# Graph attention block: bulk loading of the first chunks, query projections as jobs, and another place for the exponential

## Chip, core and metric

The kernel runs on one core of one Trainium2 chip. The metric is the device time of one execution in microseconds (us), the median over several runs. Each engine (PE for matrix products, DVE, ScalarE = ACT, GpSimd = POOL, and SP, which here only issues transfers) has a queue of its own and takes its instructions strictly in the order in which the program wrote them; semaphores hold an instruction until what it needs is there.

## What is computed

Eight frames of 2048 nodes with 256 channels go through one attention block in which a node sees only its neighbours, all in float32:

```python
qkv = einsum('fnc,ck->fnk', x, w_qkv); q, k, v = split(qkv, 3)     # 8 heads of 32 channels
scores = einsum('fnhd,fmhd->fhnm', q, k) / sqrt(32)
scores = where(adj > 0, scores, -1e9)                              # adj: 2048 x 2048, the same for all frames and heads
t = einsum('fhnm,fmhd->fnhd', softmax(scores), v)
y = layernorm(x + t);  z = relu(y @ w1 + b1) @ w2 + b2
out = layernorm(x + layernorm(y + z))
```

## The kernel before

**Tiles and items.** A frame is cut in 4 chunks of 512 queries (`qc`), the heads in 2 groups of 4 (`g`), the keys in 16 blocks of 128 (`mb`). The main loop (L418) runs over the 8 x 4 x 2 x 16 = 1024 items (f, qc, g, mb), one step for each. The 16 steps of one (f, qc, g) are here called a group; there are 64.

**One item.** `scores` (L202) takes a buffer `pt` of 128 x 4 x 512 from the pool `pp` (10 buffers) and two of three pairs of PSUM banks, issues the score products of four heads (L210, PE), adds the mask (L213, DVE, two instructions of 128 x 1024) and takes the exponential in place (L215, ACT, one instruction of 128 x 2048). `values` (L219) multiplies with V (L227, PE) into a bank `O` that collects a whole group; at the last item of a group it copies that bank to SBUF (L231, ACT). `add_up` (L240) sums the exponentials for the softmax denominators, six items of a group on POOL (L247) and six by accumulating transfers that POOL issues (L244). Scores run two items ahead: step t issues `scores(items[t + 2])`, then `values(items[t])`, then `add_up(items[t])` (L431 to L439).

**Jobs.** All other work of the loop comes as generators in the list `fill`, ordered by a due step (`start`, L368). At every step but the first of a group, `advance` (L373) lets them go on before the scores are issued, in order of their due steps; in a step only one piece of work that needs a PSUM bank is allowed (`yield BANK`), `yield n` puts a job off by n steps, and a job that loads waits until so many of the three input buffers (`live`, L96) are free; where one waits for them, no job behind it may load. The bank that a job gets (`bank`, L85) is, in the main loop, the one of two that the running group does not use as `O`: after a group's end that is the bank that L231 empties. The jobs are: the mask of the next query chunk (`mask_ahead`, L394, built of `turn_mask`, L113, in the first frame only; later frames reload masks), the turn of x for the next frame (`turn`, L148: load, transpose, store the turned chunk `xT` to DRAM as `XD`, project the queries), K and V (`project`, L176, which reloads `XD`), denominators (L271), outcome (L300) and tail (L319: layer norms and the two dense layers, with L328, L339, L349, L351).

**The start.** Before the loop, for each chunk c of frame 0 (L405): `turn` (with its queries), `project` for heads 0 to 3, `turn_mask`, which loads the adjacency block in two halves, converts each on DVE (L122), transposes (L132) and evicts with a minimum (L133). These take their buffers from the three input buffers. Then `project` for heads 4 to 7 for all chunks, from `xT` reloaded from `XD` (L182), and the scores of the first two items.

**Constants.** Weights, bias columns and rows are loaded from ACT's queue (L597 to L605) ahead of everything else on it. The identity matrix for the transposes is made on POOL (L619), which also adds two rows (L617). In this part, outside of `fast_path`, the framework may order instructions of an engine by when their operands are there; in `fast_path` the program's order stands.

Of the kernel before, what the change touches and what calls it, by code (L numbers as in the profile page):

```python
# [10 lines left out]
F32 = mybir.dt.float32  # L11
BF16 = mybir.dt.bfloat16
I32 = mybir.dt.int32
F8 = mybir.dt.float8e5
AF = mybir.ActivationFunctionType
ALU = mybir.AluOpType
AX = mybir.AxisListType

P = 128
H = 8  # L20
D = 32
CH = 512
# [6 lines left out]
BANK, TURNED, ROOM, INPUTS = -1, -2, -3, -10  # L29
# [24 lines left out]
def fast_path(ctx, tc, cst, x, adj, out, RS):  # L54
# [30 lines left out]
    def bank(dt=F32):  # L85
        shape = [P, CH] if dt == F32 else [P, 2, CH]
        if state["side"] is not None:
            i = 1 - state["side"]
            return ps_x[i].tile(shape, dt, name=f"x{i}")
        i = state["turn"]  # L90
        state["turn"] = (i + 1) % 5
        pool = ps_s[i] if i < 3 else ps_x[i - 3]
        return pool.tile(shape, dt, name=f"s{i}" if i < 3 else f"x{i - 3}")
# [4 lines left out]
    def take(shape, dt):  # L98
        live.pop(0)
        live.append(ld.tile(shape, dt, name="in"))  # L100
        return live[-1]

    def give(t):
        live[:] = [None if u is t else u for u in live]
# [8 lines left out]
    def turn_mask(qc, mc):  # L113
        if mc == 0:
            MK[0, qc] = mkp.tile([P, MB, CH], F8, name="mask")
        yield INPUTS - 3
        cv = take([P, TPC, CH], BF16)
        ts = [take([P, 2, CH], I32) for _ in range(2)]
        for half, t in enumerate(ts):
            q0 = qc * CH + half * 2 * P  # L120
            nc.sync.dma_start(t, adj[q0:q0 + 2 * P, mc * CH:(mc + 1) * CH].rearrange("(j p) m -> p j m", p=P))
            nc.vector.tensor_scalar(cv[:, 2 * half:2 * half + 2, :], t, 0.0, MASKED, op0=ALU.is_le, op1=ALU.mult)  # L122
            give(t)
            yield 1
        yield 1
        for half in range(2):
            yield BANK
            ps = bank(BF16)
            for r in range(2):
                for j in range(TPC):  # L130
                    rr = 2 * half + r
                    nc.tensor.transpose(ps[:, r, j * P:(j + 1) * P], cv[:, j, rr * P:(rr + 1) * P], identb)  # L132
            nc.vector.tensor_tensor(MK[0, qc][:, mc * TPC + 2 * half:mc * TPC + 2 * half + 2, :], ps,  # L133
                                    cst["ones"][:, 0:1, None].to_broadcast([P, 2, CH]), ALU.min, saturate=False)
        give(cv)
        if mc == NCK - 1:
            nc.sync.dma_start(MD[qc], words(MK[0, qc]))

# [5 lines left out]
    QT, KT, V, XT = {}, {}, {}, {}  # L144
    XD = [dp.tile([NCK, P, 2, CH], F32, name=f"xd{f}") for f in range(F)]


    def turn(f, c):  # L148
        yield INPUTS - 2
        xc, xT = take([P, TPC, C], F32), take([P, 2, CH], F32)  # L150
        nc.sync.dma_start(xc, x[f, c * CH:(c + 1) * CH, :].rearrange("(j p) c -> p j c", p=P))
        yield 3
        for a in range(2):
            yield BANK
            ps = bank()
            for j in range(TPC):
                nc.tensor.transpose(ps[:, j * P:(j + 1) * P], xc[:, j, a * P:(a + 1) * P], ident)
            nc.scalar.copy(xT[:, a, :], ps)
        give(xc)
        nc.sync.dma_start(XD[f][c], xT)  # L160
        XT[f, c] = xT
        yield 1
        for g in range(2):
            yield BANK
            QT[f, c, g] = channels(qp, "qT", xT, g * P)
        give(xT)

    def channels(pool, name, xT, k0):
        ps = bank()
        for a in range(2):  # L170
            nc.tensor.matmul(ps, wqkv[:, a, k0:k0 + P], xT[:, a, :], start=(a == 0), stop=(a == 1))  # L171
        t = pool.tile([P, CH], F32, name=name)
        nc.scalar.copy(t, ps)  # L173
        return t

    def project(f, c, g, xT=None):  # L176
        if xT is None:
            while (f, c) not in XT:
                yield 1
            yield INPUTS - 1  # L180
            xT = take([P, 2, CH], F32)
            nc.sync.dma_start(xT, XD[f][c])  # L182
            yield 3
            while len(KT) < (2 * f + g) * NCK + c:
                yield 1
        yield BANK
        KT[f, c, g] = channels(kp, "kT", xT, C + g * P)
        yield BANK
        ps = bank()
        for j in range(TPC):  # L190
            for a in range(2):
                nc.tensor.matmul(ps[:, j * P:(j + 1) * P], xT[:, a, j * P:(j + 1) * P],  # L192
                                 wqkv[:, a, 2 * C + g * P:2 * C + (g + 1) * P], start=(a == 0), stop=(a == 1))
        v = vp.tile([P, TPC, P], F32, name="v")
        nc.scalar.copy(v, ps.rearrange("p (j c) -> p j c", c=P))
        V[f, c, g] = v
        give(xT)
# [4 lines left out]
    def scores(item):  # L202
        f, qc, g, mb = item
        pt = PT[item] = pp.tile([P, 4, CH], F32, name="p")
        ps2 = [score_pair() for _ in range(2)]

        for half in (1, 0):
            for j in range(2):
                r = D * (2 * half + j)
                nc.tensor.matmul(ps2[half][:, j, :], KT[f, mb // TPC, g][r:r + D, (mb % TPC) * P:(mb % TPC + 1) * P],  # L210
                                 QT[f, qc, g][r:r + D, :], start=True, stop=True)
        for half, ps in enumerate(ps2):
            nc.vector.tensor_tensor(pt[:, 2 * half:2 * half + 2, :], ps,  # L213
                                    MK[f, qc][:, mb, None, :].to_broadcast([P, 2, CH]), ALU.add)
        nc.scalar.activation(pt, pt, AF.Exp, scale=1.0 / math.sqrt(D))  # L215

    LAST = MB - 1

    def values(item):  # L219
        f, qc, g, mb = item  # L220
        grp = (f, qc, g)
        if mb == 0:
            i = state["side"]
            O[grp] = ps_x[i].tile([P, CH], F32, name=f"x{i}")
        for h in range(4):
            r = D * h
            nc.tensor.matmul(O[grp][r:r + D, :], V[f, mb // TPC, g][:, mb % TPC, r:r + D], PT[item][:, h, :],  # L227
                             start=(mb == 0), stop=(mb == LAST))
        if mb == LAST:
            OT[grp] = op.tile([P, CH], F32, name=f"oT{g}")  # L230
            nc.scalar.copy(OT[grp], O.pop(grp))  # L231
# [162 lines left out]
    def mask_ahead(qc):  # L394
        for mc in range(NCK):
# [6 lines left out]
    NEXT = {(1, 1): [(turn, 0)], (3, 1): [(turn, 1)], (3, 10): [(project, 0, 0)], (5, 1): [(turn, 2)],  # L402
            (5, 8): [(project, 1, 0)], (6, 0): [(turn, 3)], (6, 4): [(project, 2, 0)], (6, 8): [(project, 3, 0)],
            (6, 12): [(project, 0, 1)], (7, 0): [(project, 1, 1)], (7, 4): [(project, 2, 1)], (7, 8): [(project, 3, 1)]}
    for c in range(NCK):  # L405
        for _ in turn(0, c):
            pass
        for _ in project(0, c, 0, XT[0, c]):
            pass
        for _ in turn_mask(0, c):  # L410
            pass
    for c in range(NCK):
        for _ in project(0, c, 1):
            pass
    state["side"] = 0
    for k in range(LEAD):
        scores(items[k])
    for t, (f, qc, g, mb) in enumerate(items):  # L418
        if mb == 0 and t:
            state["side"] = 1 - state["side"]  # L420
        if f == 0 and g == 0 and mb == 0 and qc + 1 < NCK:
            start(t, mask_ahead(qc + 1), t + 28)
        if g == 1 and mb == 0 and (f or qc == NCK - 1) and (f + 1 < F or qc + 1 < NCK):
            load_mask(f + (qc + 1) // NCK, (qc + 1) % NCK)
        if f + 1 < F:
            for what, *which in NEXT.get((2 * qc + g, mb), []):
                due = t + MB // 2 if what is turn else items.index((f + 1, 0, which[1], which[0] * TPC)) - LEAD - 1
                start(t, what(f + 1, *which), due)
        if mb:
            advance(t, 1)  # L430
        if t + LEAD < len(items):  # L431
            nf, _, ng, nmb = items[t + LEAD]
            t0 = t
            while (nf, nmb // TPC, ng) not in V:
                advance(t0, 1)
                t0 += 1
            scores(items[t + LEAD])
        values(items[t])
        add_up(items[t])  # L439
        if mb == LAST:  # L440
            start(t + SUM, denominator(f, qc, g), t)
# [129 lines left out]
def kernel(  # L571
# [26 lines left out]

    def row_of(pool, name, v):
        t = cst[name] = pool.tile([P, C], F32, name=name)  # L600
        nc.scalar.dma_start(t, bass.AP(tensor=v.tensor, offset=v.offset, ap=[[0, P], [1, C]]))

    def cols_of(name, v):
        t = cst[name] = const.tile([P, 2], F32, name=name)
        nc.scalar.dma_start(t, v.rearrange("(a p) -> p a", p=P))  # L605

    weight("wqkv", w_qkv)
    weight("w1s", w1)
# [73 lines left out]
```

## Time and profile before

| | |
|---|---|
| median of 10 runs | 3766.64 us (3761.16 to 3773.55) |
| the profiled execution: its time | 3762.37 us |
| its span in the trace | 3760.6 us |
| mean granted TensorE clock | 0.975 |
| PE busy from 94 to 563 us / granted clock there | 371.9 us of 469 / 0.91 |
| PE busy from 1032 to 1500 us / granted clock there | 418.4 us of 468 / 1.00 |
| first product of the third item (loop proper) | 98.42 us |
| last copy of a group's output (L231) in frame 0, in frame 2 | 602.24 us, 1508.84 us |

Times are microseconds from the start of the span unless marked ns. A line of the timeline has the start, the time it took, the engine, the program line, the operation, output <- input, how many instructions were merged, and in brackets the idle time before it and what ended it. "PEld" is the weight load of PE, "issue" is idle time for which the profile shows no wait. A busy PE is not PE at its peak, since the ends of pipelined products are modelled. Idle time of an engine that nothing waits for costs nothing.

### The profile page before, as it was taken

How to read it: one execution, taken by the hardware profiler on the slowest of the kernel's cores; microseconds unless marked ns; L12 is line 12 of the kernel's file. 1: busy time of each engine (PE TensorE's matmuls, PEld its weight loads, DVE VectorE, ACT ScalarE, POOL GpSimd, SP SyncE). 2: the span in 40 equal slices, each digit the busy share in tenths (PEclk: the TensorE clock that was granted, in tenths of full speed). 3: DMA queues.
4: the chain of work that ended last, by engine and by line, in shares of the span. 5: the costliest groups of instructions: out<-in, count | busy, mean ns of one | idle time of the engine just before them, and what ended most of it. 6: DMA issues, size and time to landing. Idle time of an engine off the chain costs nothing. (4 is left out here: it accounts for less than half of the span.)

```text
span 3760.6 us, 53803 instructions
## 1 busy us (share of the span) xinstructions
PE 3239.0 (86%) x22020; PEld 1044.3 (28%) x22020; DVE 2760.0 (73%) x3207; ACT 2412.1 (64%) x1921; POOL 2594.2 (69%) x1355
## 2 busy tenths in 40 slices
PE   6778788988988999888998889988898898988884
PEld 4222223222322223222332223322232222322221
DVE  1886776777678776887667886777767777688882
ACT  2555555667667666666667766666766766677673
POOL 0455656678677777777757876677767777678775
PEclk8898999999999999999999999999999999999997
DMA  5665767677667767666757776667776776777663
GB/s 150 151 157 129 164 154 163 136 158 173 157 135 168 160 143 178 146 151 151 180 138 161 166 152 159 149 151 160 157 169 134 163 164 143 175 145 149 148 135 80
DMA packets 115181, 573.84 MB, mean 153 GB/s; under 512 B 11632, under 2 KB 29168, under 8 KB 61680
## 3 DMA queue, kind: packets, MB, share of 16 engines
q0 software_dynamic: 64512, 436.24, 57.6%
q1 hardware_dynamic: 48064, 132.13, 10.1%
q8 instruction: 174, 2.85, 0.3%
q10 hardware_dynamic: 2352, 1.97, 0.3%
q14 instruction: 79, 0.65, 0.0%
HBM read 129.90 MB, written 37.75 MB: 45 GB/s over the span
## 5 line engine op out<-in xcount | busy, mean ns | idle before, releaser
L213 DVE TENSOR_TENSOR p<-s,mask 128x1024 f32<-128x1024 f32 x2048 | 2410.2, 1219 | 748.5 <-PE s L210 480.9
L215 ACT ACTIVATE p<-p 128x2048 f32<-128x2048 f32 x1024 | 1957.1, 1911 | 1215.1 <-DVE p L213 893.4
L247 POOL TENSOR_TENSOR p<-p 128x2048 f32<-128x2048 f32 x384 | 1835.6, 4819 | 669.8 <-ACT p L215 661.3
L210 PE MATMUL s<-qT,kT 32*128 32x512 f32 x8192 | 1184.9, 648 | 238.1 <-DVE p L213 237.7
L227 PE MATMUL x<-p,v 128*32 128x512 f32 x8192 | 1106.7, 613 | 0.0
L244 POOL DMA_DIRECT2D p<-p x384 | 382.0, 1015 | 360.4 <-ACT p L215 143.4
L210 PEld LDWEIGHTS s<-qT,kT 32*128 32x128 f32 x8192 | 323.7, 185 | 856.8 <-DVE p L213 702.5
L227 PEld LDWEIGHTS x<-p,v 128*32 128x32 f32 x8192 | 161.9, 108 | 789.5 <-issue 630.2
L171 PE MATMUL x<-in,wqkv 128*128 128x512 f32 x476 | 237.8, 623 | 25.3 <-ACT oT L231 10.2
L265 ACT ACTIVATE y<-y,nb,rs 128x256 f32<-128x256 f32 x384 | 224.8, 589 | 38.3 <-POOL nb L262 38.3
L281 PE MATMUL x<-p,ones 128*32 128x512 f32 x2048 | 244.3, 595 | 2.4 <-DVE y L351 0.9
L254 DVE BATCH_NORM_STATS2 st<-y 128x6 f32<-128x256 f32 x384 | 160.0, 417 | 27.3 <-DMA y<-in_x_dram 27.3
L349 PE MATMUL x<-w2s,hT 128*128 128x256 f32 x512 | 127.6, 392 | 45.7 <-ACT oT L231 42.3
L339 PE MATMUL x<-turned,w1s 128*128 128x512 f32 x256 | 130.5, 633 | 20.7 <-ACT hT L340 19.2
L171 PEld LDWEIGHTS x<-in,wqkv 128*128 128x128 f32 x476 | 82.4, 192 | 186.6 <-issue 71.0
L192 PE MATMUL x<-wqkv,in 128*128 128x128 f32 x960 | 122.9, 281 | 6.4 <-ACT kT L173 6.3
L192 PEld LDWEIGHTS x<-wqkv,in 128*128 128x128 f32 x960 | 112.4, 192 | 57.1 <-ACT kT L173 32.0
L349 PEld LDWEIGHTS x<-w2s,hT 128*128 128x128 f32 x512 | 92.0, 189 | 112.8 <-ACT oT L231 68.6
L351 DVE TENSOR_TENSOR y<-x,y 128x512 f32<-128x512 f32 x64 | 44.3, 692 | 96.6 <-PE x L349 95.9
L281 PEld LDWEIGHTS x<-p,ones 128*32 128x32 f32 x2048 | 63.7, 110 | 164.7 <-issue 128.6
L259 POOL TENSOR_TENSOR rs<-rs,mhalf 128x4 f32<-128x4 f32 x96 | 99.3, 1035 | 8.0
L122 DVE TENSOR_SCALAR in<-in 128x1024 bf16<-128x1024 int32 x32 | 35.6, 1114 | 87.1 <-DMA in<-in_adj_dram 74.4
(69 smaller groups left out, 1427.8 us busy)
## 6 DMA issues: line engine op xcount, KB each, us to landing
p<-p POOLq DMA_DIRECT2D x384, 1024.0 KB, 9.7
y<-in_x_dram POOLq DMA_DIRECT2D x64, 512.0 KB, 6.1
in<-xd SPq DMA_DIRECT2D x60, 512.0 KB, 7.5
mask<-md SPq DMA_DIRECT2D x28, 1024.0 KB, 6.6
in<-in_x_dram SPq DMA_DIRECT2D x32, 512.0 KB, 6.7
xd<-in SPq DMA_DIRECT2D x32, 512.0 KB, 9.6
in<-in_adj_dram SPq DMA_DIRECT2D x32, 512.0 KB, 5.5
out_dram<-y SPq DMA_DIRECT2D x32, 512.0 KB, 3.0
```

The costliest lines, as they stand in the source:

```text
L171: nc.tensor.matmul(ps, wqkv[:, a, k0:k0 + P], xT[:, a, :], start=(a == 0), stop=(a == 1))
L192: nc.tensor.matmul(ps[:, j * P:(j + 1) * P], xT[:, a, j * P:(j + 1) * P], wqkv[:, a, 2 * C + g * P:2 * C + (g + 1) * P], start=(a == 0), s ...
L210: nc.tensor.matmul(ps2[half][:, j, :], KT[f, mb // TPC, g][r:r + D, (mb % TPC) * P:(mb % TPC + 1) * P], QT[f, qc, g][r:r + D, :], start=Tr ...
L213: nc.vector.tensor_tensor(pt[:, 2 * half:2 * half + 2, :], ps, MK[f, qc][:, mb, None, :].to_broadcast([P, 2, CH]), ALU.add)
L215: nc.scalar.activation(pt, pt, AF.Exp, scale=1.0 / math.sqrt(D))
L227: nc.tensor.matmul(O[grp][r:r + D, :], V[f, mb // TPC, g][:, mb % TPC, r:r + D], PT[item][:, h, :], start=(mb == 0), stop=(mb == LAST))
L244: nc.gpsimd.dma_start(PT[f, qc, g, chain[0]], PT.pop(item), accum_op=ALU.add)
L247: nc.gpsimd.tensor_tensor(first, first, PT.pop(item), ALU.add)
L254: nc.vector.bn_stats(st, t[:, j, :])
L265: nc.scalar.activation(t[:, j, :], t[:, j, :], AF.Identity, bias=nb[:, j:j + 1], scale=rs[:, j:j + 1])
L281: nc.tensor.matmul(ps[r:r + D, :], cst["ones"], term[:, h, :], start=(n == 0), stop=(n == 3))
L349: nc.tensor.matmul(ps[:, (j - jj) * C:(j - jj + 1) * C], hT[:, d, j * P:(j + 1) * P], w2s[:, d, :], start=(d == 0), stop=(d == 1))
```

## The change

The start becomes one generator, `begin`. It takes all ten buffers of `pp`: four for the adjacency columns of query chunk 0 (four blocks of 512 x 512), two for the converted blocks, four for x (half of each for the chunk as loaded, half for `xT`). It issues all eight loads first. Then, for each chunk, one conversion of the whole block, the transposes, the store to `XD`, for chunk 0 the queries, K and V of heads 0 to 3, and the mask blocks. Then it issues scores and exponentials of the first two items, and after them K and V of heads 4 to 7, from the `xT` that still lies in its buffer. The queries of chunks 1 to 3 of frame 0 become jobs (`ask`), due three steps before the chunk's first item, that reload `XD`.

In the main loop the exponential of item t + 2 is issued behind `values(items[t])`, and no longer at the end of `scores`. The loads of bias columns and rows go to POOL's queue. `turn_mask`, `turn` and `project` are split into parts that `begin` and `ask` call; what they do in the loop stays as it was.

```diff
 def turn_mask(qc, mc):
...
-        give(cv)
+        yield from mask_blocks(qc, mc, cv)
+        give(cv)
...
+    def queries(f, c, xT):
+        for g in range(2):
+            yield BANK
+            QT[f, c, g] = channels(qp, "qT", xT, g * P)
...
+    def reload(f, c):
+        while (f, c) not in XT:
+            yield 1
+        yield INPUTS - 1
+        xT = take([P, 2, CH], F32)
+        nc.sync.dma_start(xT, XD[f][c])
+        yield 3
+        return xT
...
 def scores(item):
...
-        nc.scalar.activation(pt, pt, AF.Exp, scale=1.0 / math.sqrt(D))
+
+    def exponentials(item):
+        nc.scalar.activation(PT[item], PT[item], AF.Exp, scale=1.0 / math.sqrt(D))
...
-    for c in range(NCK):
-        for _ in turn(0, c):
-            pass
-        for _ in project(0, c, 0, XT[0, c]):
-            pass
-        for _ in turn_mask(0, c):
-            pass
-    for c in range(NCK):
-        for _ in project(0, c, 1):
-            pass
+    def begin():
+        flat = [pp.tile([P, 4, CH], F32, name="p").rearrange("p a q -> p (a q)") for _ in range(NCK + NCK // 2)]
+        cols = [t.bitcast(I32).rearrange("p (j m) -> p j m", m=CH) for t in flat[:NCK]]
+        cv = [t[:, i * 2 * CH:(i + 1) * 2 * CH].bitcast(BF16).rearrange("p (j m) -> p j m", m=CH)
+              for t in flat[NCK:] for i in range(2)]
+        rows = [pp.tile([P, 4, CH], F32, name="p") for _ in range(NCK)]
+        for c in range(NCK):
+            xc = rows[c][:, 0:2, :].rearrange("p a (b c) -> p (a b) c", c=C)
+            nc.sync.dma_start(xc, x[0, c * CH:(c + 1) * CH, :].rearrange("(j p) c -> p j c", p=P))
+            nc.sync.dma_start(cols[c], adj[0:CH, c * CH:(c + 1) * CH].rearrange("(j p) m -> p j m", p=P))
+        MK[0, 0] = mkp.tile([P, MB, CH], F8, name="mask")
+        for c in range(NCK):
+            nc.vector.tensor_scalar(cv[c], cols[c], 0.0, MASKED, op0=ALU.is_le, op1=ALU.mult)
+            xT = rows[c][:, 2:4, :]
+            yield from turn_rows(rows[c][:, 0:2, :].rearrange("p a (b c) -> p (a b) c", c=C), xT)
+            nc.sync.dma_start(XD[0][c], xT)
+            XT[0, c] = xT
+            if c == 0:
+                yield from queries(0, 0, xT)
+            yield from project(0, c, 0, xT)
+            yield from mask_blocks(0, c, cv[c])
+        for k in range(LEAD):
+            scores(items[k])
+            exponentials(items[k])
+        for c in range(NCK):
+            yield from project(0, c, 1, rows[c][:, 2:4, :])
+
+    def ask(f, c):
+        xT = yield from reload(f, c)
+        yield from queries(f, c, xT)
+        give(xT)
+
+    for _ in begin():
+        pass
+    for c in range(1, NCK):
+        start(0, ask(0, c), 2 * MB * c - LEAD - 1)
     state["side"] = 0
-    for k in range(LEAD):
-        scores(items[k])
...
             scores(items[t + LEAD])
         values(items[t])
+
+        if t + LEAD < len(items):
+            exponentials(items[t + LEAD])
         add_up(items[t])
...
     def row_of(pool, name, v):
...
-        nc.scalar.dma_start(t, bass.AP(tensor=v.tensor, offset=v.offset, ap=[[0, P], [1, C]]))
+        nc.gpsimd.dma_start(t, bass.AP(tensor=v.tensor, offset=v.offset, ap=[[0, P], [1, C]]))
...
     def cols_of(name, v):
...
-        nc.scalar.dma_start(t, v.rearrange("(a p) -> p a", p=P))
+        nc.gpsimd.dma_start(t, v.rearrange("(a p) -> p a", p=P))
```

More of the change, by code (lines that the diff above doesn't have):

```diff
@@ L125, in turn_mask, with mask_blocks @@
         yield 1
+        yield from mask_blocks(qc, mc, cv)
+        give(cv)
+    def mask_blocks(qc, mc, cv):
         for half in range(2):
@@ L145, in fast_path, with turn_rows @@
     XD = [dp.tile([NCK, P, 2, CH], F32, name=f"xd{f}") for f in range(F)]
[L148 to L152, printed above, removed]
+    def queries(f, c, xT):
+        for g in range(2):
+            yield BANK
+            QT[f, c, g] = channels(qp, "qT", xT, g * P)
+    def turn_rows(xc, xT):
         for a in range(2):
@@ L158, in turn @@
             nc.scalar.copy(xT[:, a, :], ps)
+    def turn(f, c):
+        yield INPUTS - 2
+        xc, xT = take([P, TPC, C], F32), take([P, 2, CH], F32)
+        nc.sync.dma_start(xc, x[f, c * CH:(c + 1) * CH, :].rearrange("(j p) c -> p j c", p=P))
+        yield 3
+        yield from turn_rows(xc, xT)
         give(xc)
@@ L162, in turn @@
         yield 1
-        for g in range(2):
-            yield BANK
-            QT[f, c, g] = channels(qp, "qT", xT, g * P)
+        yield from queries(f, c, xT)
         give(xT)
@@ L174, in channels @@
         return t
+    def reload(f, c):
[4 more added lines that the diff above has]
+        nc.sync.dma_start(xT, XD[f][c])
+        yield 3
+        return xT
     def project(f, c, g, xT=None):
         if xT is None:
[L178 to L183, printed above, removed]
+            xT = yield from reload(f, c)
             while len(KT) < (2 * f + g) * NCK + c:
@@ L404, in fast_path @@
             (6, 12): [(project, 0, 1)], (7, 0): [(project, 1, 1)], (7, 4): [(project, 2, 1)], (7, 8): [(project, 3, 1)]}
-    for c in range(NCK):
-        for _ in turn(0, c):
-            pass
-        for _ in project(0, c, 0, XT[0, c]):
-            pass
-        for _ in turn_mask(0, c):
-            pass
-    for c in range(NCK):
-        for _ in project(0, c, 1):
-            pass
+    def begin():
[25 more added lines that the diff above has]
+    def ask(f, c):
+        xT = yield from reload(f, c)
+        yield from queries(f, c, xT)
+        give(xT)
[3 more added lines that the diff above has]
+        start(0, ask(0, c), 2 * MB * c - LEAD - 1)
     state["side"] = 0
-    for k in range(LEAD):
-        scores(items[k])
     for t, (f, qc, g, mb) in enumerate(items):
```

## The prediction

> **What bounds the kernel now.** I read the page first, for the shares and for the groups that wait.
>
> ```profile
> PE 3239.0 (86%) x22020; PEld 1044.3 (28%) x22020; DVE 2760.0 (73%) x3207; ACT 2412.1 (64%) x1921; POOL 2594.2 (69%) x1355
> L213 DVE TENSOR_TENSOR p<-s,mask 128x1024 f32<-128x1024 f32 x2048 | 2410.2, 1219 | 748.5 <-PE s L210 480.9
> ```
>
> A step of the main loop is one item: its scores and its value product keep PE busy for 2.2 us, its two mask additions keep DVE busy for 2.44 us (two of 1219 ns). A bare step is therefore set by DVE, and a step with a job in it by PE, since a job adds about 2 us of PE time. Between the start and the end both sorts alternate, so time that PE loses in a step with a job is lost for good. I then looked at the start, in the timeline:
>
> ```profile
> 7.43 1.94 PE L157 MATMUL s<-ident,in 128*128 128x128 f32 x8 [7.43 <-DMA in<-in_x_dram]
> 10.40 1.07 ACT L158 COPY in<-s 128x512 f32<-128x512 f32 x2
> 11.04 3.78 PE L171 MATMUL s<-in,wqkv 128*128 128x512 f32 x4 [1.66 <-ACT in L158]
> ...
> 77.25 3.75 PE L171 MATMUL s<-in,wqkv 128*128 128x512 f32 x4 [7.92 <-DMA in<-xd]
> ...
> 98.42 2.09 PE L210 MATMUL s<-qT,kT 32*128 32x512 f32 x8 [1.35 <-DVE p L213]
> ```
>
> PE begins at 7.4 us, and the third item's scores, with which the loop proper begins, go out at 98.42. In between PE stands: up to 94 us it is busy for 63. It waits for adjacency blocks (each half is loaded when a buffer is free, about every 15 us for one chunk), for the copies of x that come back from DRAM (7.92 us), and it runs at half speed after each stop: four instructions of L171 take 3.78 us here and 1.88 us at full clock. The loads do not fill the transfer engines; a stretch of the first us in which several are queued shows what they can do (the last two columns are the DMA share and GB/s):
>
> ```profile
> 5.00:6.00 1.00, 0.00 (x0) 0.00 (x0) 0.00 (x0) 0.00 (x0) 0.00 (x0) 1.00 1.01 395
> 34.00:36.00 2.00, 0.29 (x4) 0.10 (x2) 0.00 (x0) 0.58 (x1) 0.00 (x0) 1.00 0.56 95
> ```
>
> Third, who waits for L231, the ScalarE copy that takes a finished group's output out of its PSUM bank, and one such place in the timeline:
>
> ```profile
> L231 ACT COPY oT<-x x64: 566/567/585, 162.8 to 3690.1; 128x512 f32<-128x512 f32 x64
>   PE x L349: 42.3, 29
>   PE x L171: 10.2, 7
>   PE x L132: 4.3, 3
> ```
>
> ```profile
> 1272.76 1.14 PE L210 MATMUL s<-qT,kT 32*128 32x512 f32 x8 [0.41 <-DVE p L213]
> 1273.83 1.07 PE L227 MATMUL x<-p,v 128*32 128x512 f32 x8
> 1273.92 1.91 ACT L215 ACTIVATE p<-p 128x2048 f32<-128x2048 f32 x1 [2.11 <-DVE p L213]
> 1275.74 0.57 ACT L231 COPY oT<-x 128x512 f32<-128x512 f32 x1
> 1276.36 1.99 PE L349 MATMUL x<-w2s,hT 128*128 128x256 f32 x8 [1.46 <-ACT oT L231]
> 1278.28 0.31 PEld L210 LDWEIGHTS s<-qT,kT 32*128 32x128 f32 x8 [0.33 <-issue]
> ```
>
> The group's last value product is done by 1272.4 and ScalarE is idle for 2.11 us then (up to 1273.92), but the copy stands behind the exponential of the item two ahead, which has to wait for DVE. The first job of the next group may only write in the bank that the copy frees, so PE stands for 1.46 us. That happens at 29 + 7 + 3 = 39 of the 64 group ends, 42.3 + 10.2 + 4.3 = 56.8 us in all.
>
> **What the Trainium skill says.** "TensorE: Matmul & The Clock Gate", section "What's actually happening": the array's default state is half clock, and sustained activity releases it. The trace agrees (3.78 against 1.88 us for the same four; at the first stage the change comes some 5 us after PE got going, against the page's 3.4). "DMA: Bandwidth & Descriptors", section "Issuing engines are not separate DMA queues": starting transfers from another engine saves only the issue time on the sequencer. That bears on the constants that go from ScalarE's queue to GpSimd's: here an issue of these costs 0.33 to 0.92 us on ScalarE. The same page, section "SWDGE vs HWDGE vs iDMA": GpSimd computes the descriptors in software; in this trace its issues take 1015 ns on average (L244).
>
> **Part by part.**
>
> (a) The constants' eight loads (three columns, five rows) go to POOL. ScalarE's queue is free after the three weights, at 2.3 instead of 9.1 us, so its table load (1.28) is over before x has landed. But they stand ahead of the identity matrix, made on POOL, and nothing keeps them from being issued first: 8 x about 1.1 us on top of 0.7, then 0.5 for the identity, gives about 10 us for PE's first transpose instead of 7.43. The first projection, which began at 11.04 because ScalarE's copies began at 10.40, then begins at about 12.0. Bounds: -1.5 us (POOL does the identity first) to +6 us (the identity also stands behind the sum at L617, which ran at 15.66). I take +1.
>
> (b) All x and adjacency chunks at once: 4 x (0.5 + 1) MiB and 1.25 MiB of weights, 7.6 MB, at 395 GB/s take 19 us, with some 5 us more for the small packets of the constants (from 10 to 14 us the transfer engines are full at 65 to 69 GB/s): the last has landed at about 28 us. PE's work then paces the stage. A chunk costs 8 transposes at 0.165 (1.3), K 1.88, V 1.95, 16 mask transposes (1.25): 6.4 us, and about 0.6 for the copy that stands between transposes and projection, 7.0. DVE has 1.4 + 2.4 = 3.8 for it beside that, ScalarE 2.3. The first chunk has the queries of chunk 0 too (3.76), and half clock to about 17 us costs 2.6. From 12.0: first chunk to 12.0 + 3.76 + 1.88 + 1.95 + 1.25 + 2.6 = 23.4, three more to 44.5. The first scores need a bank that the last mask eviction frees: 46.4; the second item's wait for the first addition as now, to 49.3. The four projections of heads 4 to 7, now from chunks that still lie in SBUF, take 4 x 3.83 = 15.3, and the mask additions and exponentials of the two items run beside them: to 64.7. So the third item's scores go out at about 65 instead of 98.4: **-33 us**, bounds -38 and -26 (with (a)).
>
> (c) The queries of chunks 1 to 3 become jobs. Following the queue's rules: in steps 1 to 18 the next mask's jobs (due 28) hold the input buffers; at step 19 the turn of the next frame (due 25) takes two of the three and the first query job (due 29) the third. Banks of steps 19 to 21 go to the denominator, 22 to 25 to the turn, and 26 to 31, which have no job now, to the six query projections. No other job moves, and the first query is done four steps before it is needed. What a bare step and a step with such a projection last can be read where the turn's queries stand ahead of just these steps:
>
> ```profile
> 186.30 1.98 PE L171 MATMUL x<-in,wqkv 128*128 128x512 f32 x4
> 190.28 1.98 PE L171 MATMUL x<-in,wqkv 128*128 128x512 f32 x4
> 194.74 1.14 PE L210 MATMUL s<-qT,kT 32*128 32x512 f32 x8 [0.41 <-DVE p L213]
> 197.28 1.14 PE L210 MATMUL s<-qT,kT 32*128 32x512 f32 x8 [0.41 <-DVE p L213]
> ```
>
> 190.28 - 186.30 = 3.98 against 2.54: 6 x 1.44 = **+8.6 us**. Their ScalarE copies (0.57) fit in its idle time. Each also issues a load of 0.5 MiB on SP. The adjacency loads of steps 33 and 34, which now wait in SP's queue from 186.7 on and land early, then find the buffers taken until steps 27 to 31. A load takes 5.5 us to land, two steps about 7, so DVE may stand for the conversion, which is ahead of the additions on its queue: 0 to 10 us with a spell of half clock, as such stops cost now (waits of 4 to 8 us at L122). I take **+3**.
>
> (d) The exponential behind the value product. No instruction is added and PE's and DVE's order stays. Only at the 64 group ends does ScalarE's order change: copy, then exponential. The copy waits for the value product, behind it stands the exponential of two items ahead, and behind that the next step's. The product ends 1.06 us after the scores, the copy 0.6 later; the exponential has to wait for 2.36 us of additions anyway. So the copy costs nothing while that cover stands (at half clock the product takes 1.9, and it would cost some 0.2 us). At 1276.36 the job would start at 1274.9, as the next product needs nothing later; DVE's and ScalarE's next waits are for PE, so they move along. The same job in mid-group makes a step of 4.02 us (1266.20 to 1270.22) against 5.52 here. Full gain 56.8; POOL's additions at the group's end have 9 us of slack behind them, so little should be given back. I take **-55**, bounds -60 and -20.
>
> Sum: -33 + 8.6 + 3 - 55 = -76.4. The profiled execution lasted 3762.4 (span 3760.6 and 1.8 around it), 4.3 below the median of 3766.6; I take the difference off the median: 3690.
>
> **Rivals.**
> 1. The copies come early, but PE meets the next wait, DVE's additions or a p buffer that POOL and its accumulating transfers hold (DVE waits 25.4 us for those now, 21 times). For it: DVE is the slower engine of bare steps. Against: each of the 39 places is followed by steps in which PE has no gap. Gain of (d) then about 20: 3725.
> 2. The start gains little: identity late, loads slowed by each other, adjacency waits in the first frame with half clock. (a) to (c) then give about -3 in place of -21: 3708.
> 3. Slower: the exponential comes to wait for PE. If the copy or the product, not DVE, ends last before an exponential, the value product of two steps on is late too, in a closed loop. The product now ends 1.2 us ahead of the additions; the loop decides only from there on. A loss of 0.15 us a step over 1024 steps would be 154, less 21 for the start and no gain of (d): 3899. I see no such wait in the trace.
> 4. More than thought: the first frame's 504 us (against 444 later) shrink as well because its half-clock spells go: 3665.
>
> **How the numbers follow.** Forecast 0.66 (own range 3674 to 3708), rival 1 0.14, rival 2 0.11, rival 3 0.02, rival 4 0.05, and 0.02 that everything cancels (within 0.2%, 7.5 us, about what a measurement tells from no change). The range of 3668 to 3724 leaves out half of rival 1 and most of 3 and 4. Faster 0.96, same 0.02, slower 0.02.
>
> **What would show it.** Right: third scores at about 65 us; L182 in steps 26 to 31 with six more L171 groups; no PE wait on the copy (56.8 down to under 5); copy ahead of the exponential at 64 ends. Wrong: first transposes after 14 us; PE's waits for DVE at L210 up by about as much as the copy's go down; ScalarE's exponential waiting for L227; more half clock in the first 470 us than 0.91.

## The result and the profile after

The changed kernel takes **3682.36 us** (median of 8 runs, 3674.57 to 3689.91) against 3768.82 us for the kernel before beside it: a ratio of 0.9773, 95% interval 0.9764 to 0.9782. The forecast was 3690 us. The profiled execution took 3677.56 us for a span of 3675.8, 84.8 us less than the span before.

The page of the changed kernel (line numbers have moved: L213 is now L226, L215 is L230, L349 is L364):

```profile
PE 3224.9 (88%) x22020; PEld 1037.9 (28%) x22020; DVE 2756.2 (75%) x3203; ACT 2415.0 (66%) x1921; POOL 2599.4 (71%) x1363
L226 DVE TENSOR_TENSOR p<-s,mask 128x1024 f32<-128x1024 f32 x2048 | 2410.1, 1219 | 734.8 <-PE s L223 464.4
L364 PE MATMUL x<-w2s,hT 128*128 128x256 f32 x512 | 129.4, 396 | 3.1 <-ACT hT L355 1.8
```

PE and DVE do the same work as before in all but a few instructions. L364 sat idle for 3.1 us; before, the same products waited 42.3 us for the copy of the group's output. PE's account explains the gain almost whole: its waits sum to 416.8 us against 487.2 (copies of a group's output 56.8 less, transfers 9.1, DVE 3.5, the rest 1.1), and its 22020 products were busy for 14.1 us less, together 84.5 us. The products are the same, but the array spent less time at half clock: 152.7 us of the span against 189.5, by the clock records of the two traces.

The start, in the timeline of the changed kernel:

```profile
5.82 0.57 POOL L644 DMA_DIRECT2D b2r<-in_L_gnn_b_dram  x1
6.35 0.25 POOL masks.py:197 MEMSET ident<- 128x128 f32 x1
7.84 1.94 PE L160 MATMUL s<-ident,p 128*128 128x128 f32 x8 [7.84 <-DMA p<-in_x_dram]
9.60 3.56 PE L180 MATMUL s<-p,wqkv 128*128 128x512 f32 x4
...
19.61 1.23 DVE L433 TENSOR_SCALAR p<-p 128x2048 bf16<-128x2048 int32 x1 [12.22 <-DMA p<-in_adj_dram]
...
60.54 1.14 PE L223 MATMUL s<-qT,kT 32*128 32x512 f32 x8
```

The third item's scores go out at 60.54 us instead of 98.42, 37.9 us earlier. A group's end, at the same place of frame 2 that the prediction showed. First the group's last value product in the kernel before, whose copy began only at 1275.74 us:

```profile
1271.29 1.07 PE L227 MATMUL x<-p,v 128*32 128x512 f32 x8
```

Then the changed kernel:

```profile
1228.59 1.06 PE L242 MATMUL x<-p,v 128*32 128x512 f32 x8
1229.72 0.58 ACT L246 COPY oT<-x 128x512 f32<-128x512 f32 x1 [0.60 <-PE x L242]
1230.06 1.14 PE L223 MATMUL s<-qT,kT 32*128 32x512 f32 x8 [0.41 <-DVE p L226]
1231.13 1.06 PE L242 MATMUL x<-p,v 128*32 128x512 f32 x8
1231.22 1.91 ACT L230 ACTIVATE p<-p 128x2048 f32<-128x2048 f32 x1 [0.92 <-DVE p L226]
1232.13 1.99 PE L364 MATMUL x<-w2s,hT 128*128 128x256 f32 x8
1234.05 1.14 PE L223 MATMUL s<-qT,kT 32*128 32x512 f32 x8
```

The copy follows the value product at once, and ScalarE still waits 0.92 us for DVE before the exponential. The job begins when the next value product has ended, with no gap. The step, from scores to scores, takes 3.99 us; in the kernel before it took 5.52.

Where the time went is read from the starts of the exponentials, taken one by one from the two timelines (third exponential, then frame by frame from one third exponential to the next; the last row runs to the last exponential):

| stretch | before, us | after, us | difference |
|---|---|---|---|
| to the third exponential | 102.97 | 64.14 | -38.8 |
| frame 0 | 500.0 | 506.1 | +6.0 |
| frames 1 to 6, each | 442.9 to 463.6 | 435.7 to 456.5 | -6.6 to -9.4 |
| frame 7 | 393.6 | 387.6 | -6.0 |

The start gives its 38.8 once; each later frame, with some five waits for the copy, gives about 7.6; the first frame takes 6 back.

### The profile page after: what moved, and what is told of

It is laid out like the page before. It is cut to its first block, busy times and chain, and to the rows that moved or that the text cites. A ratio compares the mean times of both kernels' runs of the same rounds, so it can differ in the third digit from the quotient of the medians.

```text
span 3675.8 us, 53762 instructions
## 1 busy us (share of the span) xinstructions
PE 3224.9 (88%) x22020; PEld 1037.9 (28%) x22020; DVE 2756.2 (75%) x3203; ACT 2415.0 (66%) x1921; POOL 2599.4 (71%) x1363
## 5 line engine op out<-in xcount | busy, mean ns | idle before, releaser
L226 DVE TENSOR_TENSOR p<-s,mask 128x1024 f32<-128x1024 f32 x2048 | 2410.1, 1219 | 734.8 <-PE s L223 464.4
L230 ACT ACTIVATE p<-p 128x2048 f32<-128x2048 f32 x1024 | 1957.1, 1911 | 1145.5 <-DVE p L226 809.6
L180 PE MATMUL x<-in,wqkv 128*128 128x512 f32 x472 | 235.6, 622 | 14.1 <-ACT turned L344 6.0
L364 PE MATMUL x<-w2s,hT 128*128 128x256 f32 x512 | 129.4, 396 | 3.1 <-ACT hT L355 1.8
L205 PE MATMUL x<-wqkv,in 128*128 128x128 f32 x896 | 114.9, 281 | 6.3 <-ACT kT L182 5.9
L205 PEld LDWEIGHTS x<-wqkv,in 128*128 128x128 f32 x896 | 104.2, 191 | 55.1 <-ACT kT L182 38.3
L364 PEld LDWEIGHTS x<-w2s,hT 128*128 128x128 f32 x512 | 93.1, 192 | 68.8 <-ACT hT L355 29.1
L343 PE MATMUL x<-ident,y 128*128 128x128 f32 x256 | 47.6, 297 | 54.6 <-ACT turned L344 39.1
L371 POOL TENSOR_TENSOR y<-y,be2r 128x1024 f32<-128x1024 f32 x32 | 93.0, 2905 | 0.2
```

The costliest lines, as they stand in the source:

```text
L230: nc.scalar.activation(PT[item], PT[item], AF.Exp, scale=1.0 / math.sqrt(D))
L364: nc.tensor.matmul(ps[:, (j - jj) * C:(j - jj + 1) * C], hT[:, d, j * P:(j + 1) * P], w2s[:, d, :], start=(d == 0), stop=(d == 1))
```

## The experiments

Ratios are to the kernel before on the same chip, with 95% intervals.

**One part alone: the exponential.** The kernel before with

```diff
-        nc.scalar.activation(pt, pt, AF.Exp, scale=1.0 / math.sqrt(D))      # end of scores
...
     for k in range(LEAD):
         scores(items[k])
+        exponentials(items[k])
...
         values(items[t])
+        if t + LEAD < len(items):
+            exponentials(items[t + LEAD])
```

> The kernel before with one part of the change alone: the exponential of item t + 2 behind the value product of item t; start, queries and constants stay as they were. Theory (PE waits for a bank whose copy stands behind an exponential): 39 waits of 1.46 us go, nothing takes their place, 3768 - 55 = about 3713 us, and PE's idle time before L349, L171 and L132 put down to the copy falls from 56.8 to under 5 us. Rival (given back): PE meets DVE's additions or a held p buffer instead, gain about 20, 3748 us. Second rival (the loop's gain in the full change came from elsewhere): 3768 us.

Measured: 3700.06 us against 3762.41, ratio 0.9832 (0.9816 to 0.9849), 62 us less. PE's waits for the copy are gone and its other waits have hardly moved: for DVE 263.4 us in all (259.3 before), for ScalarE otherwise 152.1 (153.0), most of it for copies. The rival of a gain given back falls. The profile's span is 67.0 us shorter, 10 more than the waits; 13.7 us of it is PE's busy time, which fell from 3239.0 to 3225.3 us for the same products: the array was at half clock for 165.8 us of the span and not for 189.5. That time scatters, by 10 us between the two profiles of the version with the exponential behind the jobs (159.1 and 169.1, further down).

**The other part alone.** The changed kernel with

```diff
             scores(items[t + LEAD])
+            exponentials(items[t + LEAD])
         values(items[t])
-        if t + LEAD < len(items):
-            exponentials(items[t + LEAD])
```

> The changed kernel with the exponential back at the end of the scores: only the start, the query jobs and the queues of the constants are changed. Theory: third item's scores at about 60.5 us as in the full change (38 us earlier), frame 0 about 12 us longer for six query jobs and one longer adjacency wait, nothing in frames 1 to 7: 3768 - 27 = about 3741 us, with the 56.8 us of waits for the copy back. Rival (the earlier start shifts DMA and job phases in the later frames too): 3725 us or less, frames 1 to 7 shorter by 2 us each or more.

Measured: 3741.81 us, ratio 0.9945 (0.9927 to 0.9962), 21 us less (14 to 27); by its profile, of an execution of 3733.95 us, 28.4 us of span less. The waits for the copy are back at 56.9 us, and frames 1 to 7 together last 3084 us against 3081 before. The early start moves nothing that could be told in the later frames. The two parts add up: 1.68% and 0.55% are 2.23%, the whole change is 2.27%.

**Taking the job away instead of the wait.** The kernel before with

```diff
         if mb:
-            advance(t, 1)
+            advance(t, 0 if f and mb == 1 else 1)
```

> The kernel before; in frames 1 to 7 no job may use a bank in the second step of a group, the step in which the waits for the copy fall. The exponential stays ahead of the copy; the jobs that stood in that step go to later steps. Theory (it is the bank wait that costs, not the order as such): the waits of frames 1 to 7, 34 x 1.46 = 50 us, go, while each job costs its own time wherever it stands: about 3720 us. Rival (what helps is that the exponential or the copy comes at another time on ScalarE): no gain, 3768 us, or slower if jobs come late and have to be forced.

Measured: 3745.28 us, ratio 0.9947 (0.9930 to 0.9964): 17 us, a third of the forecast, so neither side had it right. Its profile is of an execution of 3755.63 us, whose span is only 7.1 us shorter than before. There the copy's waits are down from 56.8 to 6.3 us, but PE waits more for DVE (282.6 us against 259.3), for transfers (29.5 against 18.0, most of it the reloads of L171) and for other copies (160.0 against 153.0): 41.8 us of the 50.5 come back. That the jobs which left this step crowd elsewhere is a likely reason, not a shown one. The edit changes more than the wait and does not settle the size; the next run does better.

**More of the same wait.** The kernel before, with the copy one step later:

```diff
             scores(items[t + LEAD])
+        if t and mb == 0:
+            copy_out(items[t - 1][:3])
         values(items[t])
+        if t == len(items) - 1:
+            copy_out((f, qc, g))
...
-        if mb == LAST:                                    # in values; the two lines become copy_out
-            OT[grp] = op.tile([P, CH], F32, name=f"oT{g}")
-            nc.scalar.copy(OT[grp], O.pop(grp))
```

> The kernel before, with the wait made larger instead of taken away: the copy of a finished group's output is issued one step later, behind the exponential of the next step. Theory (the first job of a group waits for that copy): the copy comes about 2.6 us later at each group end, and PE's wait grows by as much at the 39 places where a job stands there: 3766 + 100 = about 3866 us, the idle time put down to the copy up from 57 to about 160 us. Rival (the order of copy and exponential is nothing by itself): within 10 us of 3766 us.

Measured: 3951.19 us, ratio 1.0488 (1.0455 to 1.0520). The wait grew as forecast, to 116.8 + 28.2 + 13.5 = 158.5 us at 40 places, but the time by 184.5, not by 100. One place shows why:

```profile
1342.39 0.57 ACT L232 COPY oT<-x 128x512 f32<-128x512 f32 x1
1343.01 3.78 PE L350 MATMUL x<-w2s,hT 128*128 128x256 f32 x8 [4.03 <-ACT oT L232]
1346.73 1.99 PE L210 MATMUL s<-qT,kT 32*128 32x512 f32 x8
```

PE stands for 4.03 us in place of 1.46, and then the same eight products take 3.78 us instead of 1.99 and the scores 1.99 instead of 1.14: the array has fallen to half clock (granted clock 0.50 from 1342 to 1346 us). "TensorE: Matmul & The Clock Gate", section "What's actually happening", puts the fall at an idle window of about 3.4 us; 4.03 us and 1.46 us lie on its two sides, and in the kernel before no product was slower after any of the 39 waits. A sharp limit the figure is not, though: in the kernel before, a wait of 2.37 us that ended at 23.41 us was followed by half clock (granted clock 0.50 from 24 to 26 us; mask transposes every 0.107 us in place of 0.056). The clock records of these traces come in pieces of 3.41 us or a multiple of it, so where in such a piece a wait falls may matter; no run here tests that. At this place the wait is 2.6 us longer and the slower products cost another 2.6. Over the whole run the waits for the copy grew by 101.7 us and PE's busy time by 84.5 (3239.0 to 3323.5), 2.1 us for each of the 40 places, with half clock for 397.4 us of the span in place of 189.5; the two sum to 186 of the 188.3 us by which the span grew. So the order of copy and job product is causal, and a wait's price depends on its length.

**The same cause elsewhere.** The changed kernel still has PE wait 152 us for ScalarE, most of it for copies: a job's copy stands behind the exponential of the step before, and the next job needs the same bank. The exponential was moved behind the next step's jobs:

```diff
         if mb:
             advance(t, 1)
+        if t and t + LEAD - 1 < len(items):
+            exponentials(items[t + LEAD - 1])
...
-        if t + LEAD < len(items):
-            exponentials(items[t + LEAD])
         add_up(items[t])
```

> The changed kernel, with the exponential of item t + 2 moved one place further: behind the jobs of step t + 1, ahead of that step's scores. The same theory carried on: a job's ScalarE copy frees the one bank that the next job needs, and it now stands behind an exponential that still waits for DVE; in the changed kernel PE waits 39 us for each of L161 and L344, 20 for L355, 17 for L298 and about 15 for other copies. Put ahead of the exponential they should cost little: 3682 - 100 = about 3582 us. Rival: the exponential comes so late (behind a projection of 2 us and its copy, and behind layer norm activations that wait for POOL, up to 15 us) that the value product two steps on waits for it: gain under 20 us, or slower than 3682 us, with PE waits for the exponential at L242 and ScalarE idle before it for a job's product.

Measured: 3558.54 us, ratio 0.9460 (0.9435 to 0.9486). The waits of PE in the changed kernel and in this one (line, what it waited for, us in total, times, longest):

```profile
PE s L223 <- DVE p L226: 244.5, 342, 9.7
PE x L160 <- ACT in L161: 39.3, 28, 1.9
PE x L343 <- ACT turned L344: 39.1, 31, 1.5
PE x L354 <- ACT hT L355: 19.8, 31, 1.4
PE x L303 <- ACT dT L298: 17.4, 64, 0.7
```

```profile
PE s L223 <- DVE p L226: 260.9, 346, 8.8
PE x L343 <- ACT y L280: 11.5, 1, 11.5
PE x L180 <- DMA in<-xd: 8.6, 5, 2.6
```

The copies have left the head of the list; of 152 us of waits for ScalarE 17 remain, while the waits for DVE rose by 12 and those for transfers by 8.5. PE's busy time is 17.0 us less, and the span fell by 129.5. The exponential that comes later holds PE's value products up for only 0.7 us.

**The parts of the start.** These four ran side by side, the changed kernel as the yardstick.

> The changed kernel once more, as the yardstick for the three runs beside it: ratio to the kernel before 0.977, about 3680 us.

Measured: 3683.42 us, ratio 0.9774 (0.9753 to 0.9795).

```diff
-        nc.gpsimd.dma_start(t, v.rearrange("(a p) -> p a", p=P))      # and the rows' loads likewise
+        nc.scalar.dma_start(t, v.rearrange("(a p) -> p a", p=P))
```

> The changed kernel with the bias columns and rows back on ScalarE's queue. Theory: ScalarE's first copy comes at 10.4 us again in place of 8.96, the third item's scores about 1.5 us later, nothing else: 1 to 2 us slower than the changed kernel. Rival (issued from GpSimd these loads slow the bulk loads or the identity matrix, as the prediction took): 1 to 3 us faster.

Measured: 3684.27 us, ratio 0.9770 (0.9748 to 0.9791), not to be told from the yardstick. The start is later by more than thought, third scores at 65.51 us against 61.47: behind the bulk loads ScalarE's queue does not get its own loads out, and PE waits 6.56 us for ScalarE's copy.

```profile
7.33 0.35 ACTq L644 DMA_DIRECT2D g1r<-in_L_gnn_ln_g_dram  x1
11.00 0.35 ACTq L644 DMA_DIRECT2D g2r<-in_L_gnn_ln_g_dram  x1
...
14.01 1.28 ACT L161 ACT_TABLE_LOAD   x1 [14.01 <-DMA g1r<-in_L_gnn_ln_g_dram]
15.30 1.07 ACT L161 COPY p<-s 128x512 f32<-128x512 f32 x2
```

Frame 0 was shorter in that profile (502.2 us; 509.7 in the yardstick's, 506.1 in the first one of the same kernel). Frame 0 scatters by as much as the start differs, so what the constants' queue is worth in the end stays open. The rival had a point: the first adjacency block, issued at 1.25 us, had landed at 10.98 us here, against 20.37 in the yardstick, whose constants come from POOL.

```diff
-            if c == 0:
-                yield from queries(0, 0, xT)
+            yield from queries(0, c, xT)
...
-    for c in range(1, NCK):
-        start(0, ask(0, c), 2 * MB * c - LEAD - 1)
```

> The changed kernel with the queries of all four chunks projected at the start, and no query jobs. Theory: the start is longer by 3 x 3.76 = 11.3 us, frame 0 shorter by the 8.9 us that the six query jobs took: 2 to 3 us slower than the changed kernel, third item's scores at about 72 us. Rival (the jobs' reloads disturb the mask loads of frame 0): frame 0 shorter by 13 us or more, 2 us faster than the changed kernel or better.

Measured: 3683.83 us, ratio 0.9782 (0.9762 to 0.9802). Third scores at 73.59 us, 12.1 later than the yardstick's, frame 0 at 494.6 us, 12 to 15 shorter than in the two profiles of the changed kernel. What the start gains by leaving the queries out, frame 0 pays. A cost of the reloads beyond the six projections' 8.9 us is possible (3 to 6 us by these profiles), but not within what the times can tell.

```diff
+        for c in range(NCK):
+            yield from project(0, c, 1, rows[c][:, 2:4, :])
         for k in range(LEAD):
             scores(items[k])
             exponentials(items[k])
-        for c in range(NCK):
-            yield from project(0, c, 1, rows[c][:, 2:4, :])
```

> The changed kernel with the first two items' scores and exponentials issued behind the projections of heads 4 to 7, at the end of the start. Theory: their waits (PE spends 6.5 us on them at 39.2 to 45.8, 2.3 of it waiting) come later but are not longer, and the third item needs DVE either way: within 2 us of the changed kernel, third item's scores at 59 us. Rival (issuing them early hides DVE's and ScalarE's work on two items): 4 to 6 us slower.

Measured: 3679.49 us, ratio 0.9763 (0.9744 to 0.9782); third scores at 58.87 us, 2.6 earlier than the yardstick's 61.47. Issuing two items' scores half way brings nothing: PE waits there for the mask eviction and for DVE, and what follows waits for DVE anyway. With this and the two runs before it, what is left for the gain of the start is the bulk loads and `xT` staying in SBUF, which no run separates: with the queries back at the start, the third exponential still comes at 77.2 us against 103.0.

**Both together.** The version with the exponential behind the jobs, alone and with scores at the end of the start (the diffs above):

> The version with the exponential behind the next step's jobs, timed again with more rounds as the yardstick for the run beside it: about 3558 us, ratio to the kernel before 0.946.

> The same version with the first two items' scores at the end of the start as well. Theory: early scores bring nothing, so 0 to 4 us faster than the run beside it. Rival (with shorter steps the early work on two items counts): 3 us slower or more.

Measured: 3563.98 us, ratio 0.9463 (0.9448 to 0.9479), and 3560.22 us, ratio 0.9449 (0.9433 to 0.9465). The second has the lowest ratio of all runs here, though the 4 us between the two lie within their intervals. Either beats the kernel before by 5.4 to 5.5% and, by the ratios, the changed kernel by 3.2 to 3.3%.

## Why the prediction was right, step by step

**(a) Constants.** Taken at +1 us, it came out at -1.4, at the lower bound: the first projection began at 9.60 us, not at 12.0 (11.04 before). The order on POOL was as assumed (loads ahead of the identity), but the eight issues took 0.56 to 0.93 us each, in all from 1.28 to 6.39, not 1.1 each; the price had been taken from the 1 MiB accumulating transfers (1015 ns). The identity was ready before x had landed.

**(b) Bulk loads.** Forecast -33 with (a), measured -37.9, just inside the bounds. Several terms were off. A chunk took 5.8 us (first projections of the last three at 23.08, 28.86 and 34.64), not 7.0: eight transposes in a row take 1.04 us and not 1.3, the 16 mask transposes 0.9 and not 1.25, and the copy behind the transposes leaves a gap of 0.24, not 0.6. Half clock ended at about 13 us, not at 17. Against that, the loads did not run as thought: SP stood at their issue until 21.6 us, as shown below, and the first adjacency block, issued at 1.24 us, had landed only at 19.6 us. That cost PE 2.52 us ahead of the first mask transposes; the later chunks found theirs there. The block's delay goes with the constants' loads on POOL, since with these on ScalarE's queue it had landed at 10.98 us.

**(c) Query jobs.** The six jobs fell in steps 26 to 31 as worked out, and lasted 8.9 us more than bare steps (forecast 8.6). The expected wait for the adjacency loads of steps 33 and 34 did not come; a longer one came in step 7 (7.84 us for the adjacency block against 3.99), which was not foreseen. That the +3 for such waits was about the size of what came is luck. In the run with the start alone frame 0 is 9.0 us longer; less what (d) gains in frame 0, that goes with the +6.0 of the table.

**(d) Exponential.** Forecast -55 by 39 waits of 1.46 us; alone it gave -62 (-1.84% to -1.51% of 3762 us, so 57 to 69), and the waits went from 56.8 us to nothing. The mechanism and the count were right. That nothing is given back was the right choice between forecast and rival 1. The gain beyond the waits goes with less time at half clock, which the forecast had at nothing; how much of that is the change and how much scatter stays open. Rival 3 did not show: no exponential of the changed kernel waits for a value product.

The sum, -76 against -85, is short mostly by (d): as medians of the part runs, (a) to (c) gave 21 us, as forecast (21.4), and (d) 62 against 55. By the profile the start gave 5 us more than forecast as well, but the times of the part runs do not resolve that. Rival 2, -3 for (a) to (c), is excluded by the run with the start alone (14 to 27 us less). Rival 4 had something in it: the granted clock in the 470 us from 60 us on was 0.93, against 0.91 before, but the first frame grew.

## What to carry to other kernels

Where one PSUM bank serves one short job after another, the copy that empties it can lie on the path of the tensor engine, as here; look which instruction stands ahead of that copy on its engine, and whether that instruction is waiting for something else. A long instruction with slack belongs behind the short ones that others wait for, as far as its own slack goes: here one place was worth 1.7%, the next 3.2%. Count a wait not by its length alone: here waits of 4.03 us cost some 2 us of slower products on top, waits of 1.46 us none.

## What was not expected of the hardware

With many large loads under way, the queue that issues them is held up. At the start of the kernel before, SP issued the loads of x and of the adjacency blocks, a few at a time, in 0.37 to 0.44 us each. In the changed kernel its issues, of 0.44 to 0.50 us at first, stretch to microseconds (the second figure), while the first adjacency block has still not landed (19.58 us):

```profile
1.79 0.50 SPq L429 DMA_DIRECT2D p<-in_x_dram  x1
2.33 2.07 SPq L430 DMA_DIRECT2D p<-in_adj_dram  x1
4.44 8.25 SPq L429 DMA_DIRECT2D p<-in_x_dram  x1
12.73 3.68 SPq L430 DMA_DIRECT2D p<-in_adj_dram  x1
```

On SP that cost little: PE waited for none of the later chunks. On ScalarE it cost ScalarE's own work: with the constants' loads on its queue behind the bulk loads, its first copy came at 15.30 us instead of 8.96; in the kernel before, with the same loads on its queue but one chunk at a time on SP, at 10.40. What holds the queue, no run shows.
